# One pair addition per attention head moved from VectorE to an accumulating DMA, score tiles in pairs, and a re-planned order

## The chip, the cores and the metric

The kernel runs on one core of one Trainium2 chip. The metric is the device time of one execution in microseconds (us), lower is better. Engines are called PE (TensorE), DVE (VectorE), ACT (ScalarE), POOL (GpSimd) and SP (SyncE).

## The reference

Two graph layers run over 16 independent batches of 1024 nodes with 256 features, all in float32, with one 0/1 adjacency matrix per batch. The first layer is attention with 8 heads of 32; the second is a pair of graph attentions with additive scores and a feed-forward block.

```python
# layer 0
q, k, v = heads(x @ Wq), heads(x @ Wk), heads(x @ Wv)      # 8 heads of 32
e = einsum('whqd,whkd->whqk', q, k)
e = where(e >= 0, e, 0.2 * e)                               # leaky relu
attn = softmax(where(adj > 0, e, NEG), axis=-1)
h = einsum('whqk,whkd->whqd', attn, v)                      # back to 256 columns
x1 = layernorm(concat([layernorm(h), x]) @ Wffn.T) + x
# layer 1: twice
Wh = h @ W                                                  # 256 x 256
e = leaky_relu(Wh @ a_top + (Wh @ a_bottom)^T)
att = softmax(where(adj > 0, e, NEG), axis=1)
h = att @ Wh
# then layernorm(x1 + h), a feed-forward 256 -> 1024 -> 256 with relu, and a second layernorm
```

## The kernel before

The program is unrolled over the 16 batches. For each batch and each of its 8 heads the score matrix is made transposed, in 8 tiles of 128 keys by 1024 queries. One such tile passes five steps:

1. PE, line 605: two matmuls of 128 x 512 fill a score tile `ps_s` in PSUM (pool `scores`, two buffers). Their operands `qs` and `ks` hold the high and low halves of the projections, stacked along the contraction.
2. ACT, line 621: `p` = 0.2 x score (in batch 0 some by DVE, line 619). `p` is a 128 x 1024 float32 tile of the pool `p`, six buffers.
3. DVE, line 623: the maximum of `p` and the score, which completes the leaky relu and gives the score buffer back.
4. ACT, line 626: the exponential, in place.
5. POOL, line 630: `p` times the 0/1 mask of the batch, in place.

PE then multiplies `p` with the 32 value columns of the head (line 645, `ps_a<-p,v`, one product for each quarter of the queries, weights 32 columns wide), and for the softmax's denominators with a tile of minus ones (line 645, `ps_a<-p,minus_ones`). Both accumulate over the 8 tiles of a head in one PSUM bank `acc`. To spare PE sums, two tiles of a pair can be added first, so that the pair needs one sum instead of two. The kernel before does so for the first two pairs of each head (`ADDED = 2`): DVE adds tile 1 to tile 0 and tile 3 to tile 2 (`add_pair`, line 675), each sum is then taken with the next pair, and the last four tiles are summed one by one. That makes 6 sums per head.

When all heads of a batch are done, `rest(b)` runs the remainder of that batch while the next batch's heads proceed: transposes (line 366), the first layer's output (lines 771 and 774), `x1` and its projections (line 803), the two graph attentions (their weights on DVE, lines 856 and 859; their products on PE, lines 894 and 919), and the feed-forward (lines 959 and 987). Projections of the batch after that (`qk_part`, `v_part`, lines 486 and 518) and its mask (lines 423 to 437) also run meanwhile. SP's and ACT's queues issue all DMAs; POOL issues none.

Every piece is a Python generator, a thread that tells what it costs (`on`), what it takes and gives back, and when it is due (`aim`). The class `Order` plays these threads through a planner: it keeps a clock for each engine, picks the next operation by due time among those that could start within 300 ns, and emits the instruction. So each engine's order is fixed at build time, by costs written in the code and by the tables of due times `EARLY` (first batches) and `AIM`. The planner adds `SWITCH` = 93 ns when PE goes between 32-column products and others, and lets operations marked `shared` on DVE and POOL exclude each other.

```python
yield on(PE=471)                          # a score tile; SWITCH is added by the planner
yield on(POOL=2098, shared=True)          # the mask
yield on(DVE=1180, shared=True)           # a pair addition
```

A second program, `general_path`, stands behind a test of the softmax sums at the end and does not run with these inputs.

Of the kernel before, what the change touches and what calls it, by code (L numbers as in the profile page):

```python
# [34 lines left out]
class Order:  # L35
# [8 lines left out]
    SWITCH = 93.0  # L44
# [4 lines left out]
    def __init__(self, **pools):  # L49
        self.clock = defaultdict(float)  # L50
        self.port = 0.0
        self.transfers = 0.0
        self.narrow = False
        self.stretch, self.done, self.half = 0, 0.0, True
        self.pools = {k: [(0.0, i) for i in range(n)] for k, n in pools.items()}
        self.slot = {}
        self.queues = defaultdict(list)
        self.events = {}
        self.waiting = defaultdict(list)
        self.active = []  # L60
        self.made = 0
        self.now = 0.0
        self.busy = defaultdict(float)
# [73 lines left out]
    def run(self):  # L137
        while self.active:
            could = []
            for th in self.active:  # L140
                costs, shared, delay, narrow = th["op"]
                best = None
                for engine, cost in costs.items():
                    ready = th["ready"] + self.HOP[engine]
                    if th.get("last", ())[:2] == (engine, th["ready"]):
                        ready -= self.HOP[engine] + self.TAIL[engine]
                    t = asked = max(self.clock[engine], ready)
                    if shared and engine in ("DVE", "POOL"):
                        t = max(t, self.port)
                    if best is None or t + cost < best[0] + best[2]:  # L150
                        best = t, engine, cost, asked
                could.append((best, th))
# [9 lines left out]
            costs, shared, delay, narrow = th["op"]  # L162
            self.active.remove(th)
            if engine == "PE":
                if narrow != self.narrow:
                    cost += self.SWITCH
                self.narrow = narrow
            end = self.clock[engine] = self.end(engine, t, cost)
            self.busy[engine] += cost
            if shared and engine in ("DVE", "POOL"):  # L170
                self.port = end
# [12 lines left out]
def on(shared=False, delay=0.0, narrow=False, **costs):  # L184
    return "on", (costs, shared, delay, narrow)
# [45 lines left out]
def unshifted_path(  # L231
# [21 lines left out]
    ADDED = 2  # L253
# [7 lines left out]
    AIM = dict(mask0=0.759, x=0.5882, x_step=0.0012, mask=0.7438, mask_step=0.0264, qk0=0.6333, qk1=0.7649,  # L261
               qk_step=0.0231, v0=0.863, v1=0.9566, v_step=0.0513, rows=-0.1328, rows_step=0.0338, first0=0.1095,
               first1=0.2264, graph0=0.0576, graph1=0.273, graph_step=0.0015, second=0.3518, second_step=0.0609,
               normed=0.8572, normed_step=0.058, ff_wait=(None, 0, 1, 0), ff=(0.6792, -0.0871, 0.5781, 0.4984),
               ff_step=0.0581, fast0=0.4431, fast1=0.9245, fast15=0.6119, lead=1.5024)

    EARLY = dict(x=0.87, x_step=0.0004, mask=0.7193, mask_step=0.0345, qk0=0.7893, qk1=0.9441, qk_step=0.0345,
                 v0=0.8496, v1=0.9733, v_step=0.0532, rows=-0.139, rows_step=-0.0236, first0=0.1365,
                 first1=-0.0311, graph0=-0.195, graph1=-0.027, graph_step=0, second=0.3474, second_step=0.0327,
                 normed=0.781, normed_step=0.02, ff_wait=(None, 0, 1, 0), ff=(0.633, 0.0209, 0.488, 0.493),  # L270
                 ff_step=0.0422)
# [6 lines left out]
    bufs = dict(misc=3, scores=2, acc=1, p=6, stacks=2, stage=2, adj=2, adjb=2, pair=18,  # L278
# [58 lines left out]
    def stats(srcs):  # L337
# [10 lines left out]
        yield on(ACT=98)  # L348
        nc.scalar.activation(rs, mv[:, :, 1], AF.Ln, bias=eps)
        yield on(ACT=98)  # L350
# [237 lines left out]
    def all_scores():  # L588
        for b in range(B):
# [4 lines left out]
            for h in range(H):  # L594
                yield wait(("stack", b, h))
                q, kk = stacks[b, h]
                for t in range(NT):
                    due = t0 + (h * NT + t) / 2 * pace(b)
                    yield aim(due, AIM["lead"] * PACE)
                    yield take("scores")  # L600
                    ps = psum.tile([P, N], FT, tag="scores", name="ps_s")
                    yield on(PE=471)
# [30 lines left out]
    def all_values():  # L633
        for b in range(B):
            for h in range(H):
# [12 lines left out]
                added = []  # L648
                for d in range(0, NT, GV):
                    last, adds = d + GV == NT, d < ADDED * GV  # L650
                    for t in range(d, d + GV):
                        yield wait(("p", b, h, t))
                    if added:
                        yield wait(("p added", b, h, d - GV))
                    yield aim(begin[b] + (h * NT + d + 2) / 2 * pace(b), SLOT)
                    ps = [probs.pop((b, h, t)) for t in range(d, d + GV)]
                    for t, p in zip(range(d, d + GV), ps):
                        yield on(PE=430, narrow=True)
                        product(v[:, t, c:c + DH], p, 0, t == 0, False)
                        yield aim(begin[b], BIG)  # L660
                    if adds:
                        yield start(add_pair(b, h, d, ps), begin[b] + (h * NT + d + 2) / 2 * pace(b))
                    for p in added if adds else added + ps:
                        yield on(PE=430, narrow=True)
                        product(minus_ones, p, QN, False, last and p is ps[-1])
                        yield give("p")
                    added = ps[:1] if adds else []
# [5 lines left out]
    def add_pair(b, h, d, ps):  # L673
        yield on(DVE=1180, shared=True)
        nc.vector.tensor_tensor(ps[0], ps[0], ps[1], op=OP.add)  # L675
        yield give("p")
        yield fire(("p added", b, h, d))
# [786 lines left out]
```

## Time and profile before

| | us |
|---|---|
| median of 2 runs | 4434.69 |
| lowest and highest | 4434.45, 4434.94 |
| profiled execution, its own time | 4435.77 |
| span of the profiled instructions | 4433.9 |

| engine | busy us | share of the span |
|---|---|---|
| PE | 4267.4 | 96% |
| DVE | 3515.0 | 79% |
| ACT | 3004.8 | 68% |
| POOL | 2364.4 | 53% |

Busy time is the time in which at least one instruction of the engine is under way. Matmuls overlap in PE's pipeline, so a group's length in the timeline is longer than the distance to the start of the next group; distances between starts tell what a group costs. In groups of instructions the columns are: line, engine, operation, out<-in, shapes, count, then busy us and mean ns, then idle time of the engine just before them and what ended it. In the view of one tile, the three durations are least, median and most, followed by the first and last start.

### The profile page before, as it was taken

What the parts mean: (1) busy time and instruction counts of PE and PEld (TensorE: products, weight loads), DVE (VectorE), ACT (ScalarE), POOL (GpSimd) and SP (SyncE); (2) the same over time, 40 slices, a digit from 0 to 9 for tenths busy, and PEclk for the clock granted to TensorE, in tenths of its full rate; (3) what the DMA queues carried; (4) which work ended last, traced back from release to release, by engine and by line L of the source; (5) the groups of instructions that cost most, each with busy time, mean ns of one, the idle gap of its engine ahead of it and who ended that gap; (6) DMA issues with size and microseconds to landing.
All of it is one profiled execution on the core that took longest, in us unless ns stands there. A gap on an engine that the chain in (4) does not pass through costs nothing.

```text
span 4433.9 us, 77232 instructions
## 1 busy us (share of the span) xinstructions
PE 4267.4 (96%) x30539; PEld 3082.5 (70%) x30539; DVE 3515.0 (79%) x5493; ACT 3004.8 (68%) x4488; POOL 2364.4 (53%) x1033
## 2 busy tenths in 40 slices
PE   8888999999999999999999999999999999999899
PEld 4455667677676776767777676776767777677687
DVE  6877878888788888888878788887788878788853
ACT  6656675676867667676676867667676676867632
POOL 5746464464736536473564736537464564736600
PEclk9999999999999999999999999999999999999999
DMA  5413223232222322222232222322323232221100
GB/s 181 124 53 87 74 72 87 70 93 70 87 79 70 93 67 83 83 83 82 65 95 73 86 79 70 94 67 77 84 81 88 63 96 74 86 79 41 34 20 20
DMA packets 156286, 344.86 MB, mean 78 GB/s; under 512 B 21750, under 2 KB 24332, under 8 KB 155916
## 3 DMA queue, kind: packets, MB, share of 16 engines
q1 hardware_dynamic: 112140, 260.13, 20.5%
q10 hardware_dynamic: 43776, 79.71, 6.3%
q8 instruction: 243, 3.98, 0.4%
q14 instruction: 127, 1.04, 0.1%
HBM read 239.09 MB, written 100.66 MB: 77 GB/s over the span
## 4 chain that ended last, share of the span: by engine, by line
PE 67%; DVE 28%; ACT 3%; issue 2%; POOL 0%; DMA 0%; ACTq 0%; SPq 0%; DVEq 0%; POOLq 0%
PE ps_a L645 15%; PE ps_s L605 10%; PE ps_m L894 9%; PE ps_m L919 8%; DVE att L856 7%; DVE att L859 6%; DVE p L623 5%; PE ps_m L959 4%; PE ps_m L486 4%; PE ps_m L987 3%; PE ps_m L771 3%; PE ps_m L803 2%; PE ps_m L774 2%; ACT p L621 2%; PE ps_m L366 1%
## 5 line engine op out<-in xcount | busy, mean ns | idle before, releaser
L630 POOL TENSOR_TENSOR p<-p,mask 128x1024 f32<-128x1024 f32 x1024 | 2363.6, 2332 | 1837.8 <-ACT p L626 1338.2
L623 DVE TENSOR_TENSOR p<-p,ps_s 128x1024 f32<-128x1024 f32 x1024 | 1220.1, 1215 | 344.5 <-ACT p L621 336.6
L626 ACT ACTIVATE p<-p 128x1024 f32<-128x1024 f32 x1024 | 1082.2, 1059 | 301.1 <-DVE p L623 256.4
L621 ACT ACTIVATE p<-ps_s 128x1024 f32<-128x1024 f32 x1006 | 996.0, 1020 | 198.2 <-PE ps_s L605 91.9
L605 PE MATMUL ps_s<-qs,ks 128*128 128x512 f32 x2048 | 684.7, 439 | 50.6 <-DVE p L623 46.6
L645 PE MATMUL ps_a<-p,v 128*32 128x256 f32 x8192 | 559.2, 388 | 12.2 <-POOL p L630 12.2
L605 PEld LDWEIGHTS ps_s<-qs,ks 128*128 128x128 f32 x2048 | 337.1, 190 | 276.2 <-issue 116.5
L894 PE MATMUL ps_m<-y,att 128*128 128x258 f32 x2048 | 484.6, 382 | 5.5 <-ACT y L864 1.9
L919 PE MATMUL ps_m<-y,att 128*128 128x256 f32 x2048 | 480.9, 381 | 1.8 <-ACT y L864 1.8
L959 PE MATMUL ps_m<-rT,wf 128*128 128x256 f32 x2048 | 472.6, 381 | 7.1 <-ACT z L324 2.4
L987 PE MATMUL ps_m<-wf,hid 128*128 128x256 f32 x2048 | 473.8, 380 | 1.3 <-ACT xT L324 1.1
L894 PEld LDWEIGHTS ps_m<-y,att 128*128 128x128 f32 x2048 | 386.4, 190 | 76.7 <-ACT hid L968 6.1
L645 PE MATMUL ps_a<-p,minus_ones 128*32 128x256 f32 x6144 | 407.9, 383 | 31.8 <-DVE p L675 31.5
L959 PEld LDWEIGHTS ps_m<-rT,wf 128*128 128x128 f32 x2048 | 379.6, 190 | 69.8 <-ACT hid L968 8.1
L987 PEld LDWEIGHTS ps_m<-wf,hid 128*128 128x128 f32 x2048 | 379.3, 190 | 59.1 <-issue 7.6
L919 PEld LDWEIGHTS ps_m<-y,att 128*128 128x128 f32 x2048 | 379.7, 190 | 55.8 <-ACT y L864 2.6
L645 PEld LDWEIGHTS ps_a<-p,v 128*32 128x32 f32 x8192 | 213.4, 109 | 288.7 <-issue 155.2
L675 DVE TENSOR_TENSOR p<-p 128x1024 f32<-128x1024 f32 x256 | 374.1, 1461 | 18.2 <-PE ps_a L645 16.8
L856 DVE SCALAR_TENSOR_TENSOR att<-first,second 128x1024 f32<-128x1024 f32 x256 | 370.1, 1446 | 13.5 <-ACT first L843 13.5
L859 DVE SCALAR_TENSOR_TENSOR att<-mask,att 128x1024 f32<-128x1024 fp8e4 x256 | 343.8, 1343 | 7.7
L645 PEld LDWEIGHTS ps_a<-p,minus_ones 128*32 128x32 f32 x6144 | 199.0, 111 | 172.4 <-DVE p L675 41.3
L864 ACT ACTIVATE y<-y,check 128x258 f32<-128x258 f32 x256 | 130.6, 510 | 247.6 <-DVE check L862 246.4
(106 smaller groups left out, 4427.8 us busy)
## 6 DMA issues: line engine op xcount, KB each, us to landing
qs<-qk_halves SPq DMA_DIRECT2D x256, 256.0 KB, 3.7
ks<-qk_halves SPq DMA_DIRECT2D x256, 256.0 KB, 5.1
adj_i<-in_adj_dram ACTq DMA_DIRECT2D x240, 256.0 KB, 3.2
qk_halves<-high SPq DMA_DIRECT2D x128, 256.0 KB, 2.5
qk_halves<-low SPq DMA_DIRECT2D x128, 256.0 KB, 2.9
xr<-in_x_dram ACTq DMA_DIRECT2D x64, 256.0 KB, 3.0
x_kept<-x SPq DMA_DIRECT2D x64, 256.0 KB, 2.1
x<-x_kept SPq DMA_DIRECT2D x64, 256.0 KB, 3.2
```

Of the source, the lines that this page charges most:

```text
L605: nc.tensor.matmul(ps[:, cols], kk[:, t * P:(t + 1) * P], q[:, cols], start=True, stop=True)
L621: nc.scalar.activation(p, ps, AF.Copy, scale=ALPHA)
L623: nc.vector.tensor_tensor(p, p, ps, op=OP.max)
L626: nc.scalar.activation(p, p, AF.Exp)
L630: nc.gpsimd.tensor_tensor(p, p, mask_of(b, t), op=OP.mult)
L645: nc.tensor.matmul(acc[i * DH:(i + 1) * DH, at:at + QN], w, p[:, i * QN:(i + 1) * QN], start=first, stop=last)
L856: nc.vector.scalar_tensor_tensor(e, first[:, 0, :], second[:, j:j + 1], first[:, 1, :], op0=OP.mult, op1=OP.max)
L859: nc.vector.scalar_tensor_tensor(e, mask_of(b, j), -1.0, e, op0=OP.mult, op1=OP.mult, accum_out=sums[:, j:j + 1])
L894: nc.tensor.matmul(pa[:, cols:cols + width], big[:, j, i * P:(i + 1) * P], rows[:, j, :width], start=(j == 0), stop=(j == NT - 1))
L919: nc.tensor.matmul(pa[:, i * D:(i + 1) * D], big[:, j, t * P:(t + 1) * P], y2[:, j, :D], start=(j == 0), stop=False)
L959: nc.tensor.matmul(pa[:, i * 2 * P:(i + 1) * 2 * P], wf1[:, dc, hc * P:(hc + 1) * P], rT[:, dc, :], start=(dc == 0), stop=(dc == DC - 1))
L987: nc.tensor.matmul(pa[:, i * D:(i + 1) * D], hid[hc // 2][:, hc % 2, i * P:(i + 1) * P], wf2[:, hc, :], start=(hc == 0), stop=False)
```

## The change

Four things change together.

1. Of the two pair additions of a head, the first (tiles 0 and 1) becomes a DMA issued by POOL that adds tile 1 to tile 0 in SBUF (`accum_op=OP.add`, 512 KB of source). The second (tiles 2 and 3) stays on DVE. Both sums are now taken with the third pair. There are still 6 sums per head.
2. From batch 1 on, score tiles are asked for in pairs: a thread takes both score buffers, and the second tile of a pair follows with the highest urgency.
3. The planner's costs are others: `SWITCH` becomes a table by kind of matmul, DVE and POOL exclude each other for a little less than a whole operation, and one small ACT operation costs 318 in place of 98.
4. The pool `p` has five buffers in place of six, and the due times in `AIM` and `EARLY` are others. So the order of all instructions on all engines is another.

```diff
-    SWITCH = 93.0
+    SWITCH = {(None, "narrow"): 93.0, ("single", "narrow"): 93.0, ("narrow", None): 93.0,
+              ("narrow", "single"): 197.0, (None, "single"): 84.0}
...
             if shared and engine in ("DVE", "POOL"):
-                self.port = end
+                if engine == "DVE":
+                    self.port["POOL"] = end - 54.0
+                else:
+                    self.port["DVE"] = end - 130.0
...
-    ADDED = 2
+    PAIRS = ('dma', 'dve', 'none', 'none')
+    AFTER = dict(dma=2, dve=1, none=0)
+    JOINCOST = 1100
+    JOINDELAY = 3500
...
-    bufs = dict(misc=3, scores=2, acc=1, p=6, stacks=2, stage=2, adj=2, adjb=2, pair=18,
+    bufs = dict(misc=3, scores=2, acc=1, p=5, stacks=2, stage=2, adj=2, adjb=2, pair=18,
...
-        yield on(ACT=98)
+        yield on(ACT=318)
         nc.scalar.activation(rs, mv[:, :, 1], AF.Ln, bias=eps)
...
                     due = t0 + (h * NT + t) / 2 * pace(b)
-                    yield aim(due, AIM["lead"] * PACE)
-                    yield take("scores")
+                    if b == 0 or t % 2 == 0:
+                        yield aim(due, AIM["lead"] * PACE)
+                        for _ in range(2 if b else 1):
+                            yield take("scores")
+                    else:
+                        yield aim(t0, BIG)
                     ps = psum.tile([P, N], FT, tag="scores", name="ps_s")
-                    yield on(PE=471)
+                    yield on(PE=464, mode="single")
...
-                added = []
-                for d in range(0, NT, GV):
-                    last, adds = d + GV == NT, d < ADDED * GV
...
+                late = []
+                for u in range(NP):
+                    last, how = u + 1 == NP, PAIRS[u]
+                    tiles = range(2 * u, 2 * u + 2)
+                    for t in tiles:
                         yield wait(("p", b, h, t))
-                    if added:
-                        yield wait(("p added", b, h, d - GV))
...
+                    sums = []
+                    while late and (late[0][0] <= u or last):
+                        at, what, p = late.pop(0)
+                        yield wait(("p joined", b, h, what))
+                        sums.append(p)
...
-                    if adds:
-                        yield start(add_pair(b, h, d, ps), begin[b] + (h * NT + d + 2) / 2 * pace(b))
-                    for p in added if adds else added + ps:
-                        yield on(PE=430, narrow=True)
-                        product(minus_ones, p, QN, False, last and p is ps[-1])
+                    if how == "none":
+                        sums += ps
+                    else:
+                        yield start(join(b, h, u, how, ps), due)
+                        late.append((u + AFTER[how], u, ps[0]))
+                    for p in sums:
+                        yield on(PE=430, mode="narrow")
+                        product(minus_ones, p, QN, False, last and p is sums[-1])
                         yield give("p")
...
-    def add_pair(b, h, d, ps):
-        yield on(DVE=1180, shared=True)
-        nc.vector.tensor_tensor(ps[0], ps[0], ps[1], op=OP.add)
+    def join(b, h, u, how, ps):
+        if how == "dve":
+            yield on(DVE=1180, shared=True)
+            nc.vector.tensor_tensor(ps[0], ps[0], ps[1], op=OP.add)
+        else:
+            yield on(POOL=JOINCOST, delay=JOINDELAY)
+            nc.gpsimd.dma_start(ps[0], ps[1], accum_op=OP.add)
         yield give("p")
-        yield fire(("p added", b, h, d))
+        yield fire(("p joined", b, h, u))
```

## The prediction

> **What bounds the kernel now.** I read the page first. TensorE is busy for 96% of the span and carries 67% of the chain that ended last, with VectorE at 28%.
>
> ```profile
> span 4433.9 us, 77232 instructions
> PE 4267.4 (96%) x30539; PEld 3082.5 (70%) x30539; DVE 3515.0 (79%) x5493; ACT 3004.8 (68%) x4488; POOL 2364.4 (53%) x1033
> PE 67%; DVE 28%; ACT 3%; issue 2%; POOL 0%; DMA 0%; ACTq 0%; SPq 0%; DVEq 0%; POOLq 0%
> ```
>
> Next the table by stretch. I cut it where batches 0, 1, 2, 3, 5, 6 and 15 begin their first value product (columns: length, then busy us of PE, PEld, DVE, ACT, POOL, clock, DMA share, GB/s).
>
> ```profile
> 0.00:254.20 254.20, 209.78 (x1573) 122.51 (x1573) 184.64 (x249) 170.17 (x241) 153.28 (x75) 0.95 0.49 141
> 254.20:520.00 265.80, 228.42 (x1677) 155.48 (x1677) 210.56 (x308) 173.22 (x241) 154.85 (x66) 0.93 0.26 72
> ...
> 1311.50:1578.30 266.80, 263.22 (x1907) 191.33 (x1907) 218.02 (x341) 189.15 (x283) 146.50 (x65) 1.00 0.28 80
> 1578.30:1845.10 266.80, 263.21 (x1905) 191.31 (x1904) 218.08 (x341) 189.15 (x283) 146.48 (x65) 1.00 0.28 80
> ...
> 3986.80:4433.90 447.10, 420.05 (x2635) 332.09 (x2634) 288.45 (x526) 218.25 (x378) 146.80 (x62) 0.98 0.10 29
> ```
>
> The middle of the run repeats every 266.8 us with TensorE busy for 263.2, so only 3.6 us of a batch is visible idle. The first two batches leave it idle for 82 us (254.2-209.8 plus 265.8-228.4), the last stretch for 27 us. TensorE is the bound; what counts is its own work and who makes it wait.
>
> Busy time hides what TensorE loses between kinds of matmul, so I read the timeline of PE (start, length, group):
>
> ```profile
> 2213.22 1.19 PE L605 MATMUL ps_s<-qs,ks 128*128 128x512 f32 x4
> 2214.25 1.91 PE L894 MATMUL ps_m<-y,att 128*128 128x258 f32 x8
> 2216.08 1.07 PE L645 MATMUL ps_a<-p,v 128*32 128x256 f32 x16
> 2217.08 1.20 PE L605 MATMUL ps_s<-qs,ks 128*128 128x512 f32 x4
> 2218.12 1.91 PE L894 MATMUL ps_m<-y,att 128*128 128x258 f32 x8
> 2219.86 0.60 PE L695 MATMUL ps_m<-ident,ho 128*128 128x128 f32 x4
> ...
> 2238.31 3.65 PE L894 MATMUL ps_m<-y,att 128*128 128x258 f32 x16
> 2241.89 1.07 PE L645 MATMUL ps_a<-p,v 128*32 128x256 f32 x16
> ```
>
> Start to start, 8 L894 records take 1.74 before an equal kind (2218.12 to 2219.86) and 1.83 before narrow ones. Over the whole trace I sorted the intervals by pattern: a narrow record (weights of 32 columns, L645) takes 0.0543 us, a score record (L605) 0.233. A narrow episode between wide groups costs 0.22 us on top, and 0.33 if a score pair ends it. A single score tile between wide groups costs from 0 to 0.08 (the quarter point and the median of its intervals). Summed over all records this gives 3994 us of work and 148 us of changes of kind; the other 292 us of the span are waits, 156 of them before batch 4 begins, about 9 in each repeating batch, 35 in the last.
>
> **What the Trainium skill says.** TensorEngine Tiling (Array Packing), Key Properties: changing the tiling mode drains the engine. The trace agrees in kind (0.22 us for in and out). SBUF — State Buffer, Who interferes with whom: a VectorE instruction with two SBUF inputs contends with a GpSimd one that reads SBUF, and the later one waits. The trace agrees: the pair addition takes 1190 ns at best and 3182 at worst. Collectives: The Full Stack, The bandwidth ceiling: an add in the DMA path needs two source reads per chunk. No run here shows it.
>
> **The change, part by part.**
>
> *VectorE.* 128 of 256 pair additions leave it (one per head):
>
> ```profile
> L675 DVE TENSOR_TENSOR p<-p 128x1024 f32<-128x1024 f32 x256 | 374.1, 1461 | 18.2 <-PE ps_a L645 16.8
> ```
>
> 128 x 1.461 = 187 us of VectorE, 11.7 per batch, and 128 chances to hold GpSimd's multiply (mean 2332 ns, least 2118). VectorE isn't the bound, so this pays only where TensorE waits for it. In the wait table these are the score tiles (46.6 and 91.0 us behind L623) and the sums (31.5 and 41.3 behind L675), some 210 us, part of it covered. Bounds: nothing, or half of the steady 9 us per batch (4.5 x 15 = 67). I take 1.3 us a batch, 20 us, since the two largest holes left there are chains through transposes and ScalarE.
>
> *TensorE's order.* The matmuls are the same in kind and number (6 sums per head in both). From the instruction order of both programs I counted the changes of kind: narrow to score 331 before, 150 after; narrow to wide 184, now 373; wide to score 336, now 389; narrow episodes 515, now 523. Score runs of two tiles go from 350 to 478, single tiles from 315 to 59. Gain 181 x 0.104 = 18.9; cost 8 x 0.22 = 1.8, and 53 x 0 to 0.08 = up to 4. Sum: -17 to -13, taken -15.
>
> *Pairs of score tiles.* The second of a pair waits for the maximum (L623) of the tile two before it. ScalarE, VectorE and TensorE take about 0.93 + 2 x 1.02 + 1.2 = 4.2 us for a pair. A batch has 32 pairs in 266.8 us, 8.3 each (batch 0 keeps single tiles). Queued behind that wait is everything on PE. I cost it at nothing; if the cover goes it is part of the VectorE waits above.
>
> *The accumulating DMA.* In GpSimd's order it stands behind the multiply of tile 1 or 2, and waits for TensorE's first value product of tile 0. Behind it on GpSimd stand the next multiplies. GpSimd has 266.8 - 146.5 = 120 us free per batch, and eight issues at an estimated 1 us each (DMA: Bandwidth & Descriptors, Specifications: first byte about 1 us from GpSimd) fit. Who waits for its end: PE's sum of pair 0 at the third pair; and, since p has 5 buffers instead of 6, ScalarE's L621 of tile 5, which refills tile 1's buffer. Behind that L621 all of ScalarE waits. The cover is TensorE's work between the products of pair 0 and that of tile 5. From the new order and the durations above it is, in a repeating batch, 26.0, 28.3, 12.3, 13.2, 12.5, 12.9, 15.5 and 12.9 us for heads 0 to 7. From L621 to the product, tile 5 needs 5.7 us (first starts in the view of tile p):
>
> ```profile
> L623 DVE TENSOR_TENSOR p<-p,ps_s x1024: 1184/1215/1223, 40.4 to 4198.2; 128x1024 f32<-128x1024 f32 x171
> L626 ACT ACTIVATE p<-p x1024: 1041/1059/1087, 41.7 to 4199.4; 128x1024 f32<-128x1024 f32 x171
> L630 POOL TENSOR_TENSOR p<-p,mask x1024: 2118/2147/3198, 42.8 to 4200.6; 128x1024 f32<-128x1024 f32 x171
> L621 ACT ACTIVATE p<-ps_s x1006: 1001/1023/1084, 39.4 to 4196.5; 128x1024 f32<-128x1024 f32 x168
> ```
>
> L621 at 39.4, the multiply at 42.8 plus 2.15, and 0.15 to TensorE. So the join, issue to landing, is covered up to 6.6 to 7.5 us in five heads of eight. No DMA of this kind is in the trace. Nearest rows:
>
> ```profile
> ks<-qk_halves SPq DMA_DIRECT2D x256, 256.0 KB, 5.1
> qk_halves<-high SPq DMA_DIRECT2D x128, 256.0 KB, 2.5
> x_kept<-x SPq DMA_DIRECT2D x64, 256.0 KB, 2.1
> ```
>
> Low end: 1 + 2.0 + 0.5 MB at 436 GB/s (1.2) = 4.2 us by the same DMA page, Anatomy of one DMA. With two reads, 5.4. High end: two read passes at the rate of the ks row beside other traffic, 8 to 9. I take 5.4: covered, cost 0. The plan in the code assumes 1.1 + 3.5.
>
> *Batch 0.* It is not bound by TensorE (the first value products of its heads lie 18 to 24 us apart in the trace, mean 21.1 over the first seven). There the join is in the loop: 5.4 + 5.7 to tile 5's product, 0.9 until its sum frees a buffer, then tiles 7, 0 and 1 of the next head through GpSimd (5.7 + 2 x 2.15): 22.4 us a head. 8 x 1.3 = 10 us. Bounds 0 and 30.
>
> *Sum*, against the profiled execution (4435.8 us, 1.9 over its span): -20 - 15 + 0 + 10 = -25, so 4411. The median of the runs is 1.1 below the profiled one: 4410.
>
> **The rivals.**
> 1. *The join is late* (slower). One mechanism: ScalarE's L621 of tile 5 waits for the landing, and TensorE for tile 5. It decides from about 7 us. At 8.8 us the five tight heads lose 2.2 + 1.3 + 2.0 + 1.6 + 1.6 = 8.7 us, over 14 batches 122, and batch 0 some 30 more: 4560. For it: second reads, and DMA engines at 28% already with bursts of four loads per head. Against: stores of 256 KB land in 2.1 to 2.9 us.
> 2. *The waits melt* (faster). Half the steady waits (67) and a third of the 156 us before batch 4 (50) go with the additions and the new order, with 15 from the order: 4435 - 132 = 4303. For it: VectorE's share of the chain (28%). Against: repeating batches have only 3.6 us of visible idle.
> 3. *Nothing is left.* The order's 15 us are eaten by pairs waiting for both score buffers and by batch 0: 4435.
>
> **How the numbers follow.** Forecast 0.54, late join 0.26, melted waits 0.08, nothing left 0.12. The join case spreads from 4480 up, and 8 in 10 of all lie between 4340 and 4560. A measurement of this kernel can tell about 2%, 89 us. Faster by more needs rival 2: 0.08. Slower by more (above 4523) is most of rival 1: 0.22. The rest, 0.70, is within.
>
> **What would show it.** Right: batches repeat in some 264 us; the join lands within 7 us of its issue; L675 appears 128 times; PE's waits for L623 and L675 shrink; GpSimd's multiply gets a little shorter. Wrong: L621 on ScalarE, or the sums on PE, waiting for the join for tens of us in total (rival 1); a batch period below 260 (rival 2); or batch 0's heads over 24 us apart, which would put the loss at the start.

## The result, and the profile after

The changed kernel takes 4666.41 us (median of two runs, 4664.26 and 4668.57) against 4434.69: ratio 1.0524, 95% interval 1.0503 to 1.0545. It is 5% slower, and outside the predicted range. Lines of code that moved are L605 to L615 (scores), L621 to L631, L623 to L633, L626 to L636, L630 to L640 (multiply), L645 to L655 (products and sums), L423 to L429 (cast of the mask). The pair additions, L675 before, are L693 on VectorE and L696 as the DMA.

From the page of the changed kernel, the span, busy times and the chain that ended last:

```profile
span 4666.8 us, 77354 instructions
PE 4326.5 (93%) x30539; PEld 3126.4 (67%) x30539; DVE 3322.1 (71%) x5440; ACT 2981.0 (64%) x4413; POOL 2374.9 (51%) x1161
PE 71%; DVE 15%; ACT 5%; POOL 4%; issue 4%; DMA 1%; ACTq 0%; POOLq 0%; DVEq 0%
```

VectorE lost 193 us of work, as intended, and its share of the chain fell from 28% to 15%. The span still grew by 232.9 us. TensorE has the same 30539 matmuls and is idle for 340 us in place of 166.

The table by stretch, cut again where batches 0, 1, 2, 5, 6 and 15 begin their first value product (length, busy us of PE, PEld, DVE, ACT, POOL, clock, DMA share, GB/s):

```profile
0.00:269.00 269.00, 196.42 (x1401) 100.81 (x1401) 159.82 (x169) 148.73 (x190) 147.83 (x83) 0.84 0.51 141
269.00:563.90 294.90, 236.83 (x1717) 163.50 (x1716) 205.70 (x321) 175.15 (x244) 144.95 (x73) 0.89 0.32 84
...
1414.70:1692.20 277.50, 265.26 (x1905) 193.80 (x1904) 204.15 (x339) 186.32 (x276) 149.06 (x73) 0.99 0.35 92
1692.20:1968.90 276.70, 264.47 (x1905) 193.12 (x1904) 204.80 (x339) 186.34 (x276) 149.07 (x73) 0.99 0.35 92
...
4194.50:4666.80 472.30, 433.54 (x2665) 338.81 (x2664) 290.84 (x546) 232.95 (x407) 147.36 (x70) 0.97 0.15 39
```

By the first value products of batches 4, 14 and 15, the 232.9 us are: 94.0 before batch 4 begins (1146.7 against 1052.7), 110.1 over batches 4 to 13 (2770.6 against 2660.5, so 11 a batch), 3.6 in batch 14 and 25.2 in the last stretch (472.3 against 447.1). In batch 0 the heads lie 25 to 29 us apart, the first 34; before it was mostly 18 to 24. Loss is everywhere, not in one stage. Of the 94 us before batch 4, batch 0 has 16 (222.7 us against 206.4), batch 1 has 29 and batch 2 has 49.

The DMA itself did what was expected of it. From the view of tile p:

```profile
L696 POOL DMA_DIRECT2D p<-p x128: 840/876/1100, 48.1 to 4426.5; - x128
...
  DMA p<-p: 18.5, 13
...
DMA to landing us min/median/max: 4.4/4.5/6.8
```

It is issued in 0.88 us, lands 4.5 us after its issue, and engines stood idle for it for 18.5 us in the whole run. The join is not late. GpSimd, though, stood idle for 83.4 us in front of the issue, in 42 places, until TensorE had read the tiles; its multiplies stand behind it.

What is new in the middle batches is one long hole of TensorE. From the timelines of PE, VectorE and GpSimd in batch 9 (start, length, group; in brackets the idle time before it and what ended that):

```profile
2774.12 0.59 PE L439 MATMUL ps_m<-ident_b,adj_b 128*128 128x128 bf16 x4 [4.37 <-DVE hid L986]
2774.50 6.50 PE L980 MATMUL ps_m<-rT,wf 128*128 128x256 f32 x16
...
2782.16 1.99 PE L980 MATMUL ps_m<-rT,wf 128*128 128x256 f32 x8
```

```profile
2767.47 5.15 DVE L429 TENSOR_SCALAR adj_b<-adj_i 128x512 fp8e4<-128x512 int32 x2
```

```profile
2766.87 0.88 POOL L696 DMA_DIRECT2D p<-p  x1 [1.57 <-PE ps_a L655]
2767.47 4.51 POOL L640 TENSOR_TENSOR p<-p,mask 128x1024 f32<-128x1024 f32 x2
```

The first of two casts, normally 0.42 us each, lasts until the two multiplies that run in a row behind the DMA's issue are over, so the pair takes 5.15 us. All of VectorE's queue stands behind them; TensorE waits 4.4 us, and its next 16 records take 6.50 us, where 8 of the same kind take 1.99 a moment later. The clock column (the third number from the end of a line) shows why: within 2773.5 to 2780.2 us it reads 0.50.

```profile
2773.50:2780.20 6.70, 6.08 (x18) 4.91 (x18) 3.25 (x7) 2.84 (x5) 2.12 (x1) 0.50 0.14 43
2780.30:2790.00 9.70, 9.70 (x97) 6.70 (x96) 6.08 (x9) 5.59 (x7) 4.19 (x2) 1.00 0.54 143
```

Over the whole trace I counted VectorE operations that lasted over 2.5 us more than their usual time: none before, 18 after, each behind a DMA issue, 14 of them the cast L429 (a "long hold" from here on). The half clock covers 91 us of the trace before and 291 us after.

### The profile page after: what moved, and what is told of

Same layout as the page of the kernel before. It is cut to its first block, busy times and chain, and to the rows that moved or that the text cites. A ratio compares the mean times of both kernels' runs of the same rounds, so it can differ in the third digit from the quotient of the medians.

```text
span 4666.8 us, 77354 instructions
## 1 busy us (share of the span) xinstructions
PE 4326.5 (93%) x30539; PEld 3126.4 (67%) x30539; DVE 3322.1 (71%) x5440; ACT 2981.0 (64%) x4413; POOL 2374.9 (51%) x1161
## 4 chain that ended last, share of the span: by engine, by line
PE 71%; DVE 15%; ACT 5%; POOL 4%; issue 4%; DMA 1%; ACTq 0%; POOLq 0%; DVEq 0%
PE ps_a L655 15%; PE ps_m L915 10%; PE ps_m L940 8%; PE ps_s L615 8%; PE ps_m L980 7%; PE ps_m L1008 6%; POOL p L640 4%; DVE p L633 3%; DVE att L880 3%; DVE att L877 3%; PE ps_m L492 3%; PE ps_m L792 2%; PE ps_m L795 2%; PE ps_m L372 2%; PE ps_m L824 2%
## 5 line engine op out<-in xcount | busy, mean ns | idle before, releaser
L640 POOL TENSOR_TENSOR p<-p,mask 128x1024 f32<-128x1024 f32 x1024 | 2291.3, 2256 | 1985.9 <-ACT p L636 1822.3
L633 DVE TENSOR_TENSOR p<-p,ps_s 128x1024 f32<-128x1024 f32 x1024 | 1228.0, 1215 | 546.7 <-ACT p L631 544.8
L636 ACT ACTIVATE p<-p 128x1024 f32<-128x1024 f32 x1024 | 1083.6, 1058 | 548.2 <-DVE p L633 525.2
L631 ACT ACTIVATE p<-ps_s 128x1024 f32<-128x1024 f32 x1006 | 1003.4, 1020 | 216.7 <-PE ps_s L615 116.6
L615 PE MATMUL ps_s<-qs,ks 128*128 128x512 f32 x2048 | 667.9, 443 | 64.3 <-DVE p L633 62.3
L655 PE MATMUL ps_a<-p,v 128*32 128x256 f32 x8192 | 573.7, 393 | 43.3 <-POOL p L640 41.7
L940 PE MATMUL ps_m<-y,att 128*128 128x256 f32 x2048 | 492.8, 386 | 33.6 <-ACT y L885 19.7
L980 PE MATMUL ps_m<-rT,wf 128*128 128x256 f32 x2048 | 505.1, 398 | 17.3 <-ACT hid L989 10.2
L615 PEld LDWEIGHTS ps_s<-qs,ks 128*128 128x128 f32 x2048 | 366.2, 192 | 215.9 <-issue 77.6
L1008 PE MATMUL ps_m<-wf,hid 128*128 128x256 f32 x2048 | 480.5, 382 | 18.8 <-ACT hid L989 12.2
L980 PEld LDWEIGHTS ps_m<-rT,wf 128*128 128x128 f32 x2048 | 398.3, 199 | 102.8 <-ACT hid L989 17.9
L1008 PEld LDWEIGHTS ps_m<-wf,hid 128*128 128x128 f32 x2048 | 381.6, 191 | 82.4 <-ACT hid L989 22.4
L655 PEld LDWEIGHTS ps_a<-p,v 128*32 128x32 f32 x8192 | 208.7, 110 | 314.5 <-POOL p L640 123.4
L655 PE MATMUL ps_a<-p,minus_ones 128*32 128x256 f32 x6144 | 388.5, 386 | 0.0
L877 DVE SCALAR_TENSOR_TENSOR att<-first,second 128x1024 f32<-128x1024 f32 x256 | 351.9, 1375 | 14.8 <-ACT first L864 14.1
L880 DVE SCALAR_TENSOR_TENSOR att<-mask,att 128x1024 f32<-128x1024 fp8e4 x256 | 355.1, 1387 | 4.4
L655 PEld LDWEIGHTS ps_a<-p,minus_ones 128*32 128x32 f32 x6144 | 202.1, 112 | 139.8 <-issue 13.0
L989 ACT ACTIVATE hid<-ps_m,columns 128x256 f32<-128x256 f32 x391 | 171.5, 471 | 94.5 <-PE ps_m L980 94.4
```

The source lines that it names most:

```text
L615: nc.tensor.matmul(ps[:, cols], kk[:, t * P:(t + 1) * P], q[:, cols], start=True, stop=True)
L631: nc.scalar.activation(p, ps, AF.Copy, scale=ALPHA)
L633: nc.vector.tensor_tensor(p, p, ps, op=OP.max)
L636: nc.scalar.activation(p, p, AF.Exp)
L640: nc.gpsimd.tensor_tensor(p, p, mask_of(b, t), op=OP.mult)
L655: nc.tensor.matmul(acc[i * DH:(i + 1) * DH, at:at + QN], w, p[:, i * QN:(i + 1) * QN], start=first, stop=last)
```

## The experiments

In the diffs, "+" is the experiment. Times are medians; each ratio is to the kernel before, timed beside it on the same chip, with its 95% interval. The kernel before came out between 4429.5 and 4434.8 us there, so a few us between two experiments say nothing.

### What the DMA and the long hold cost in the changed kernel's own order

**e1_no_join.** The order of all else stays; tile 1 of each head is missing from the softmax sums.

```diff
-            nc.gpsimd.dma_start(ps[0], ps[1], accum_op=OP.add)
```

> The changed kernel with the same order on every engine, but the accumulating DMA is not issued: tile 1 of a head is left out of the softmax sums. Port theory (behind the DMA's issue two multiplies on GpSimd run without a gap, VectorE's mask cast waits 4.4 us for both, TensorE runs dry and falls to half clock): no VectorE operation is held over 2.5 us, a middle batch falls from 278 to 266-268 us, the total to 4430-4500. Loop theory (tile 5 waits for the landing, with five p buffers): also fast, 4430-4500, and batch 0's heads fall from 28 to 22 us. Plan theory (pairs of score tiles and the new order cost it): stays above 4600.

Measured 4634.54, ratio 1.0454 (1.0423 to 1.0484). Above 4600, as the plan theory has it: without any DMA only 32 of the 232 us go. Batch 0's heads stay at 23 to 29 us (the first 34). The casts of the hole above still stand behind multiplies, each for some 1.9 us in place of one for 4.8:

```profile
2743.33 4.15 DVE L429 TENSOR_SCALAR adj_b<-adj_i 128x512 fp8e4<-128x512 int32 x2
```

So neither the DMA's latency nor its traffic is the main loss.

**e2_join_on_dve.** VectorE adds where the DMA was issued, in the same order.

```diff
-            nc.gpsimd.dma_start(ps[0], ps[1], accum_op=OP.add)
+            nc.vector.tensor_tensor(ps[0], ps[0], ps[1], op=OP.add)
```

> The changed kernel in its own order, with the addition put on VectorE at the place where GpSimd's queue had the DMA. Port theory: no hold over 2.5 us on VectorE, middle batches 267-271 us, total 4470-4530. Loop theory: tile 1's buffer comes free after about 1.5 us and not after 4.5, so batch 0's heads fall to 24 us and the middle batches to 270, total 4480-4550. Plan theory: above 4600.

Measured 4807.99, ratio 1.0845 (1.0813 to 1.0876), 142 us more than with the DMA, and again only the plan theory allowed it. No operation is held long here. An addition on VectorE in a place not planned for it costs this order far more than the DMA does; which waits make up the cost stays open.

**e3_cast_one_port.** The cast gives -1 times the 0/1 adjacency, in the form that also writes out an accumulator (`counted`, a new tile of one column).

```diff
-            nc.vector.tensor_scalar(..., ai, 0.0, -1.0, op0=OP.is_gt, op1=OP.mult, saturate=False)
+            nc.vector.tensor_scalar(..., ai, -1.0, None, op0=OP.mult, op1=OP.add, accum_out=counted, saturate=False)
```

> The changed kernel in its own order, DMA kept; only the mask cast on VectorE (adjacency to fp8) is written in the form with an accumulator, which by the Trainium skill's SBUF page does not take the port shared with GpSimd. Port theory: the 4.8 us casts become 0.4-0.7 us, the hole of 4.4 us in front of the mask transposes and the half clock after it go, a middle batch falls from 278 to 269-271 us, total 4560-4590. Loop theory and plan theory: 4650-4670, the same as the changed kernel.

Measured 4594.47, ratio 1.0363 (1.0333 to 1.0393): 72 us below the changed kernel, and a little above the 4590 that the port theory allowed. In the groups (busy us, mean ns), the cast of the changed kernel and then of this one:

```profile
L429 DVE TENSOR_SCALAR adj_b<-adj_i 128x512 fp8e4<-128x512 int32 x256 | 180.9, 737 | 14.1 <-DMA adj_i<-in_adj_dram 9.3 <-PE ps_m L439 4.7
```

```profile
L431 DVE TENSOR_SCALAR_CACHE_REDUCE adj_b<-adj_i 128x512 fp8e4<-128x512 int32 x256 | 174.1, 680 | 16.6 <-DMA adj_i<-in_adj_dram 9.0 <-PE ps_m L441 3.7
```

The new form is slower than a free cast (0.42) but is not held long. A middle batch falls from 278 to 271.4 us, and runs at full clock:

```profile
1683.40:1954.80 271.40, 262.90 (x1908) 191.89 (x1907) 204.10 (x355) 186.24 (x276) 148.93 (x73) 1.00 0.37 94
```

This is the form of which the Trainium skill (SBUF — State Buffer, Who interferes with whom) says that it doesn't enter the modes in which VectorE contends with GpSimd. This case agrees: 687 ns at most in this form, against 4811 ns. The page has the later of the two wait for the other's whole instruction; here a cast waited through two multiplies in a row.

**e17_no_join_cast.** Both edits, e1's and e3's, in the changed kernel's order.

> The changed kernel, in its own order, with the join's DMA not issued (tile 1 of each head is left out of the sums) and the mask's cast in the accumulator form. Alone these gave 32 and 72 us. Theory A (two separate costs): 4545 to 4580, and the 110 to 145 us over the kernel before are what the order by itself costs. Theory B (one and the same cost: without the DMA hardly a long hold is left): 4585 to 4605.

Measured 4587.94, ratio 1.0353 (1.0335 to 1.037), as the second theory has it. With the short cast, the DMA costs 6 us or nothing (the intervals overlap). The four kernels in the same order split the loss:

| | old cast | accumulator cast |
|---|---|---|
| with the DMA | 4666 (the change) | 4594 (e3) |
| without it | 4635 (e1) | 4588 (e17) |

The order by itself, with the accumulator cast, costs 4587.94 - 4434.51 = 153 us. Of the other 78, the old cast costs 47 even without the DMA, where no hold is over 2.5 us; the DMA alone costs 6; and 25 come only when both are there, through the long holds. So the 72 us of e3 are not all the DMA's: the DMA answers for 6 to 32 us, and the order, with the casts as they are, for 200. By stages (span 4588.0, batches 4, 14 and 15 starting at 1133.2, 3846.7 and 4119.4) the 154 us of this profile are 80.5 before batch 4, 53 in batches 4 to 13, -1 in batch 14 and 21.5 at the end.

**e9_six_buffers.** Five buffers are planned, six exist; every engine's order is the same.

```diff
-    work = Order(**bufs)
+    work = Order(**bufs); bufs["p"] = 6
```

> The changed kernel, every engine's instructions in the same order, with six real buffers for the score tiles in place of five (the planner still plans with five). In batch 0 of the changed kernel ScalarE's first pass waited for TensorE's products to give a buffer back, 22.0 us in 8 waits, and heads are 25 to 29 us apart. Theory A (with tile 0 held until the third pair's sums, five buffers are too few, and this slows batch 0): these waits go, the heads of batch 0 come to 25 us or less, and the kernel ends 20 to 50 us sooner, 4615 to 4645. Theory B (the distances are in the planned order itself, and the buffers only follow it): heads stay at 25 to 29, and the time stays within 10 us of 4666.

Measured 4694.73, ratio 1.0585 (1.0568 to 1.0603), so 28 us slower, which neither theory expected. ScalarE's waits for a buffer in 60 to 260 us fall from 22.0 to 12.6 us, but batch 0 gets only 4.4 us shorter (218.3 against 222.7 us), and VectorE is held over 2.5 us 29 times in place of 18. The real buffers are not what spreads the heads. That work which comes sooner met the other engine at a worse moment fits the count of holds, but no run shows it apart.

### What a new plan costs

Are the due times of the kernel before fitted to its one order? Five kernels start from it, each with a part of the change, and let the planner make a new order.

**e5_before_nudged.** One cost in the plan; the work is the same.

```diff
-                    yield on(PE=471)
+                    yield on(PE=464)
```

> The kernel before, with one number of the plan moved: a score tile is planned at 464 ns in place of 471. Nothing else; the same instructions, but from the 782nd matmul on in another order. Order theory (the due times are tuned to one plan, and any new plan with untuned due times makes new holes): 2 to 4% slower than before, 4520-4600, with repeating batches of no single period. Part theory (the DMA, the pairs or the five buffers each cost something of their own): 4425-4450, no change.

Measured 4497.1, ratio 1.0150 (1.0121 to 1.018), between the two expectations. Seven nanoseconds in the price of a score tile cost 68 us (against 4429.5), though the order is the old one up to the 782nd matmul. The middle batches no longer repeat, they take 256 to 288 us.

**e8_before_costs.** All planner prices of the change (`SWITCH`, the port, 318 for one small ScalarE operation, 105 for the next, and the 464 of e5).

> The kernel before with the plan's new costs alone (table of switches, the looser port between VectorE and GpSimd, 318 for the small ScalarE operation). If the looser port costs are to blame, 4560-4650, with more VectorE time held by GpSimd; if they are merely nearer to the chip, no slower than the nudged kernel.

Measured 4497.71, ratio 1.0152 (1.0122 to 1.0181): as the nudge. The prices cost no more than that one new order.

**e6_before_pairs.** Only the pairs of score tiles.

```diff
+                    if b == 0 or t % 2 == 0:
                         yield aim(due, AIM["lead"] * PACE)
+                        for _ in range(2 if b else 1):
                             yield take("scores")
+                    else:
+                        yield aim(t0, BIG)
```

> The kernel before with one part of the change: score tiles in pairs from batch 1 on. Six buffers, both additions on VectorE, the old costs and due times. Part theory: if pairs are what costs, 4550-4650. Order theory: about the same as the nudged kernel, within 40 us.

Measured 4521.1, ratio 1.0204 (1.0175 to 1.0234), 24 us over the nudge, as the order theory has it; the two intervals overlap a little.

**e18_before_p5.** Only `p=5`.

> The kernel before with five buffers for the score tiles in place of six, its order planned anew; nothing else is changed. Any new order with the old due times cost about 67 us (4497 with one score price nudged, and 4498 with the new prices). Theory A (five buffers are too few): 4530 to 4570. Theory B (the sixth buffer was spare): 4480 to 4510, as any new order.

Measured 4548.91, ratio 1.0252 (1.0235 to 1.0269), in the first theory's range and some 50 us over the nudge. Plans that were no fit to begin with moved by 1 to 21 us under small edits (e8 against e5, e12 and e10 below against the change), so 50 is more than that; but it is one plan, and that the sixth buffer wasn't spare is likely, not shown.

**e19_before_new_due.** Only the tables `AIM` and `EARLY` of the change.

> The kernel before with the due times of the changed kernel alone, its order planned anew; six buffers, both additions on VectorE, old prices, no pairs of score tiles. Theory A (the new due times spread the work of a batch beside the heads in a worse way): 4530 to 4580, heads of the middle batches at 26 us and more in place of 20 to 22 between the long ones. Theory B (they serve as well as any but the fitted ones): 4480 to 4510.

Measured 4593.12, ratio 1.0354 (1.0337 to 1.0371), above either range and some 95 us over the nudge, with heads mostly of 24 to 32 us between the long ones of the middle batches (20 to 22 before), as expected by the first theory. Of the parts tried alone without the DMA this is the dearest.

**e12_after_nudged.** A smaller nudge in the changed kernel: the score tile planned at 465 in place of 464 (in e5 it was 7 ns, not 1).

> The changed kernel with a score tile planned at 465 ns in place of 464 and the order planned anew; the work is the same. The same nudge took the kernel before from 4430 to 4497, since its due times fit one order. Theory A (the changed kernel's due times fit its own order as well): slower by 30 to 100 us, 4700 to 4770. Theory B (its order is one of many, not a fitted one, and what it lost is the fit): within 30 us of 4666, on either side.

Measured 4669.89, ratio 1.0529 (1.0512 to 1.0547): no different, as the second theory has it. That fits a kernel before whose due times suit one order, which a new plan leaves, and a changed one with nothing of that kind to lose; with one nudge each, and of two sizes, that isn't settled.

### What the DMA does to a plan

**e13_before_dma_in_place.** The order of the kernel before is kept. GpSimd issues the DMA where VectorE added the first pair.

```diff
-            nc.vector.tensor_tensor(ps[0], ps[0], ps[1], op=OP.add)
+            if u == 0:
+                nc.gpsimd.dma_start(ps[0], ps[1], accum_op=OP.add)
+            else:
+                nc.vector.tensor_tensor(ps[0], ps[0], ps[1], op=OP.add)
```

> The kernel before, in its own planned order, with one edit at the place of the first pair's addition: GpSimd's queue issues the accumulating DMA there, in place of VectorE's add. Nothing is planned anew, so this is the change of engine without the new order. Theory A (the loss lies in the new order; DMA and issue are cheap in themselves, 32 us in the changed kernel's order): 4420 to 4480. Theory B (the loss comes with the DMA's issue on GpSimd's queue in any order, through multiplies that then run in a row and hold VectorE): 4500 to 4570, with operations of VectorE held over 2.5 us. Theory C (the join lands late: heads in the kernel before are 20.2 us apart in places, 5 us a pair, and the sum is due at the next pair, against 4.5 us and more for the join): over 4500 too, but with TensorE's waits for the join at the sums.

Measured 4742.9, ratio 1.0706 (1.0688 to 1.0724), and this is the third theory's side. Its waits:

```profile
ACT p L628 <- DMA p<-p: 303.5, 75, 10.5
...
PEld ps_a L652 <- DMA p<-p: 158.8, 47, 8.9
...
PE ps_a L652 <- DMA p<-p: 137.6, 38, 8.4
```

No VectorE operation is held over 2.5 us here. ScalarE waits 303.5 us for the buffer that the join frees, and TensorE waits for the sum. A join of 4.8 us in the median (10.1 at most) replaces an addition of 1.2 to 1.5 us, and the old order has no room for it. The landing isn't all of it: 55 of the 128 issues come over 3 us after TensorE has read the pair, each straight behind a multiply on GpSimd's queue, and 438 of the 610 us of waits for the join are waits for these. So the DMA did not fit the old order, in time or in place, and a new order has a price of its own (e5).

**e7_before_dma.** The DMA with its sum at the third pair, planned anew with the old due times, prices and six buffers.

```diff
-    PAIRS = ('dve', 'dve', 'none', 'none')
+    PAIRS = ('dma', 'dve', 'none', 'none')
```

> The kernel before with one part of the change: the first addition of a head by the accumulating DMA, its sum taken with the third pair. Six buffers, single score tiles, old costs and due times. Port theory: operations of VectorE held over 2.5 us appear, all right behind a DMA issue, and the half clock with them; 4540-4640 and more than the nudged kernel by 20-60 us. Order theory alone: as the nudged kernel.

Measured 4751.49, ratio 1.0724 (1.0693 to 1.0756), far above what either theory allowed. ScalarE's waits for the join are down to 20.4 us, but VectorE is held over 2.5 us some 60 times, and batch 0's heads are 25 to 33 us apart. The planner hid the latency and lost as much in other places. With the DMA, the other parts of the change together (due times, pairs, prices, five buffers) are 85 us better than the old ones; without it, the new due times alone are worse (e19).

**e10_join_as_measured.** The changed kernel with the join planned as the trace shows it.

```diff
-            yield on(POOL=JOINCOST, delay=JOINDELAY)     # 1100, 3500
+            yield on(POOL=JOINCOST)                      # 900
             nc.gpsimd.dma_start(ps[0], ps[1], accum_op=OP.add)
+            yield pause(JOINDELAY)                       # 3600
```

> The changed kernel with the DMA join planned as the trace shows it: the issue 0.9 us, the sum 3.6 us after it, and no place in the planner's queue of transfers (which puts the landing at least 6.2 us after the issue starts, and holds every later transfer back by 2.9 us for each join). All else is as in the changed kernel, and the order is planned anew. Theory A (the planner's price of the join is what stretches batch 0 and the later order): batch 0's heads at 21 to 25 us, middle batches at most 275, 4540 to 4600. Theory B (the order suffers from the join's place, not from its price): any new order with these due times costs what it costs; 4640 to 4740. Theory C (only the stalls behind the DMA's issue count): within 20 us of 4666.

Measured 4687.57, ratio 1.0571 (1.0553 to 1.0589). That is the second theory's range: a cheaper join in the plan gains nothing, so the planner's price isn't the cause. ScalarE's waits for the join rise to 91.2 us.

Three plans from the changed kernel's planner, with its five buffers, pairs, prices and due times, complete a square: who adds the first pair, and at which pair its sum is taken.

**e4_replan_dve.** `PAIRS = ('dve', 'dve', 'none', 'none')`, sums at the next pair.

> The changed kernel with both additions on VectorE from the start (PAIRS with dve for the first pair), planned anew with the same due times, pairs of score tiles, five buffers. If the DMA is at the root (port or loop theory): 4420-4500, middle batches 265-269 us. If the pairs, the five buffers or the due times are at the root: above 4560.

Measured 4547.43, ratio 1.0257 (1.0224 to 1.0290), between both expectations, so neither the DMA nor the rest is the whole cause.

**e15_dve_late.** As e4, and the first pair's sum at the third pair:

```diff
-                        late.append((u + AFTER[how], u, ps[0]))
+                        late.append((u + (2 if u == 0 else 1), u, ps[0]))
```

> The changed kernel's planner and due times, with both additions on VectorE, planned anew, and the first pair's sum taken at the third pair as for the DMA. It differs from the kernel with both additions on VectorE (4547.4) only in that one step. Theory A (the sum at the third pair with five buffers keeps a tile too long, and that spreads the heads): most of the 119 us between 4547 and 4666 come back, 4620 to 4680, heads of batch 0 at 25 us and more. Theory B (the DMA on GpSimd's queue does it): 4530 to 4570, heads of batch 0 at 21 to 25 us.

Measured 4585.55, ratio 1.0342 (1.0324 to 1.036), between both expectations.

**e16_dma_early.** The DMA, with its sum at the second pair: `AFTER = dict(dma=1, dve=1, none=0)`.

> The changed kernel, planned anew, with the DMA join's sum taken at the second pair in place of the third, so that its buffer comes back a pair earlier. Theory A (the late sum costs the time): 4560 to 4620. Theory B (the DMA and its issue on GpSimd's queue cost it): 4640 to 4700. Theory C (the join comes too late for the second pair): over 4700, with TensorE waiting for the join.

Measured 4571.69, ratio 1.0318 (1.0301 to 1.0335), in the first theory's range.

| sum of the first pair | VectorE adds | DMA adds |
|---|---|---|
| at the second pair | 4547 (e4) | 4572 (e16) |
| at the third pair | 4586 (e15) | 4666 (the change) |

The DMA with an early sum is 95 us faster than the change, and its join is not late: ScalarE waits 15.7 us for it, TensorE's weight loads 5.8. VectorE is held over 2.5 us 37 times there, twice as often as in the change, so the count of long holds doesn't rank the kernels. The late sum alone costs 38, the DMA alone 24, both together 119. Since 7 ns in the plan have cost 68 us, the 24 and the 38 may be no more than what a plan happens to give; the 95 is more than either nudge gave.

**e11_before_cast.** The kernel before, in its own order, with e3's cast.

> The kernel before with the mask's cast in the accumulator form alone (680 ns in place of about 410, no long hold). Its order is the same. Theory A (the long hold is brought by the DMA's issue on GpSimd's queue, and the kernel before hardly has it: no VectorE operation is held over 2.5 us above its usual time): within 12 us of the kernel before, 4420 to 4442. Theory B (the casts suffer from the multiplies in any order): 30 us or more are gained, under 4400, and it is the version that beats both.

Measured 4450.68, ratio 1.0043 (1.0029 to 1.0057): 16 us slower, more than the first theory allowed. There was no long hold to take away, so only the dearer cast is left. No version tried beats the kernel before.

## Why the prediction was wrong

Most of the signs that it named for being right came true: the join landed within 7 us (6.8 at most), the pair addition on VectorE appears 128 times, TensorE's waits for the maximum and the additions shrank, and the mean multiply of GpSimd went from 2332 to 2256 ns. Only the batches repeat in 278 us and not 264. So the parts that it looked at were judged fairly well, and the loss came in where it had put a gain or nothing.

*VectorE.* The work removed was right (193 us against 187). The waits from which it took 20 us of gain did fall: for the maximum at the score tiles from 137.6 to 119.5 us, for the additions from 72.8 to nearly nothing. But TensorE's waits for the multiply rose by more. Before, then after:

```profile
PEld ps_s L605 <- DVE p L623: 91.0, 140, 2.3
...
PE ps_s L605 <- DVE p L623: 46.6, 84, 1.9
PEld ps_a L645 <- POOL p L630: 43.5, 67, 2.3
...
PE ps_a L645 <- POOL p L630: 12.2, 12, 1.8
```

```profile
PEld ps_a L655 <- POOL p L640: 123.4, 180, 2.9
...
PE ps_s L615 <- DVE p L633: 62.3, 39, 5.1
...
PEld ps_s L615 <- DVE p L633: 57.2, 68, 3.8
...
PE ps_a L655 <- POOL p L640: 41.7, 45, 2.4
```

The waits for the multiply are the order's and not the DMA's: e17, without it, has 123.7 and 38.8 us of them.

*The order.* This is the step that failed. The prediction gave the new order -15 us, from the changes of kind on TensorE, and took the waits of the old order as given (9 us in a middle batch, 156 before batch 4). Its count may hold: the changes of kind are in the traces as counted, and with the same durations for both kernels a middle batch has about 1 us less of TensorE work after. But waits belong to an order. Measured, the new order without the DMA and with the accumulator cast is 153 us slower (e17; some 16 of this may be the dearer cast, by e11), and with the old cast 200 (e1). In a middle batch of the changed kernel TensorE is idle for 12.2 us (276.70 less 264.47) in place of 3.6. Early on, a part of the loss stands in three holes, at 330, 405 and 720 us:

```profile
PE ps_m L940 <- ACT y L885: 19.7, 1, 19.7
...
PE ps_m L915 <- ACT y L885: 15.4, 1, 15.4
...
PE ps_m L940 <- DVE hn L723: 12.3, 1, 12.3
```

There the next operation in TensorE's order is a product of the graph attentions, and its operands aren't ready; in the first of the holes VectorE makes their weights (L877, L880) almost without a break. The kernel before has two holes of 9.5 us in these batches. Holes of 12 us and more are there in every run with the due times of the change, e17 and e19 too, and in one only of the runs with the old ones (e7). So they come with the due times, and they are some 28 of the 94 us. That the old order was a narrow fit was not weighed at all; e5, a single nudge, prices it at 68 us.

*Pairs of score tiles.* Put at nothing; 24 us over the nudge in the old plan (e6), hardly told apart from nothing.

*The DMA.* Its price was near: 5.4 us taken, 4.5 measured (the low end, without a second read, was 4.2), 0.88 us of issue against 1. That it is covered was right as well (18.5 us of waits). So the rival of the late join had the right side with a mechanism that the changed kernel doesn't show; e13 shows that mechanism in the old order, at a join of 4.8 us, far below the 7 us that the rival named for the new one, and there with issues that were late themselves. What was missed is what stands behind the issue on GpSimd's queue. The prediction asked whether the issues fit into its idle time, and not that multiplies then become ready together and run in a row, with a cast of VectorE between them. It used the skill's page for the pair addition and not for the casts. What casts lose to multiplies is 72 us with the DMA (e3) and 47 without it (e1 against e17).

*Batch 0.* 22.4 us a head were predicted, from the join's loop (the terms as written add up to 22.0), and it is about 28. Batch 0 as a whole is 16 us longer, near the 10 that were predicted and within the bounds of 0 to 30; that was luck. The loop as worked out was not the limit: without the DMA the heads stay at 23 to 29 us (e1), and with six real buffers at 24 to 29 (e9), while a plan without the DMA has them at 21 to 28 (e4). The sentence that over 24 us apart would put the loss at the start was right for 94 of 232.9 us, but most of these lie in batches 1 and 2.

*Half clock.* It was in no step. By an estimate, 200 us more of it cost at most 100 us (half, where TensorE has work throughout), a part of the same 232 and not on top. In the hole of batch 9, 4.4 us were lost by waiting and then some 2.5 us more, since 16 records took 6.50 us and not twice 1.99.

The chance of 0.22 for slower by more than 2% was too low, and no case of the four held a loss through the order itself; with e5's 68 us alone added to the forecast, it would have been 4478.

Open stays why the new due times spread the heads of the middle batches so much (e19), how the 153 us divide between due times, pairs and five buffers, and whether due times fitted anew on the chip would bring the DMA with the early sum below 4434; no such fit was tried.

## What to carry to other kernels

Where a planner fixes every engine's order, first nudge one of its constants and measure: what that costs (1.5% here) is a first price of a new order, and a change must earn more. Where an operation of 1.2 us becomes one of 4.5 us on another queue, the old order may not fit it (7% here), so test it once in the old order (who waits) and once in the new one with the operation taken out (what the order costs). And when a queue gets one more issue, look at what becomes ready behind it and runs in a row, and at which engine is held by that.

## What the runs showed of the hardware that was not expected

- An accumulating DMA within SBUF of 512 KB in float32, issued by GpSimd: 0.88 us of issue, then 4.4 us at least, 4.5 in the median and 6.8 at most to landing in the changed kernel (4.3 to 10.1 over all runs).
- A cast of 0.42 us on VectorE was held through two GpSimd multiplies in a row, to 4.81 us at most; the accumulator form of the same cast takes 0.68 us in the mean and 0.69 at most. Without long holds to take away, the accumulator form is the slower one (e11, 16 us for 256 casts).
- TensorE's clock was granted at half for 6.7 us around the end of a hole of 4.4 us. The Trainium skill (TensorE: Matmul & The Clock Gate, Part 1) has it fall to half after an idle window of about 3.4 us. The trace of the changed kernel agrees in that nearly every hole longer than that is followed by a slow stretch (21 of 22), and most slow stretches are 3.4 or 6.8 us long. But much shorter holes were followed by one too, as here at 1974.7 us, after 1.66 us:

```profile
1973.82 0.44 PE L372 MATMUL ps_m<-ident,hn 128*128 128x128 f32 x2 [1.66 <-DVE hn L366]
```

```profile
1970.00:1974.70 4.70, 3.04 (x17) 2.21 (x18) 4.70 (x10) 2.85 (x4) 3.49 (x3) 1.00 0.56 112
1974.70:1978.10 3.40, 3.40 (x9) 2.69 (x9) 3.30 (x11) 1.74 (x5) 0.00 (x0) 0.50 0.00 0
```
